# Summing the 16 states of a scan by adding DMA transfers into two tiles in turn, instead of additions on GpSimd

## Chip, cores, metric

One core of a Trainium2 chip. The time is the device time of one execution in microseconds (us); of several executions the median is given. A ratio is the mean time of one kernel's fast runs over the mean of the kernel before's fast runs of the same rounds, so it is not quite the ratio of the medians quoted.

## The reference, cut to what matters

Four images (128 channels, 64 x 64) pass through four layers: 0, attention; 1, two quantised convolutions; 2, a selective scan (Mamba) with group norm; 3, attention. The change touches the end of one step of layer 2:

```python
def step(h, inp):
    dt_t, B_t, C_t, x_t = inp
    dA = jnp.exp(dt_t[..., None] * A)                  # A: 256 channels x 16 states
    dBx = dt_t[..., None] * B_t[:, None, :] * x_t[..., None]
    h = dA * h + dBx
    y = jnp.einsum('bdn,bn->bd', h, C_t)               # the sum over the 16 states
    return (h, y)
...
y = ys + xc * D
y = y * jax.nn.silu(z)                                 # the gate
return y @ W_out
```

## The kernel before: the parts that matter

The kernel does one chunk of 512 pixels at a time, a *group* g; there are 32. In a group, states n = 0 to 15 follow each other; m = 16 g + n counts them, 512 in all. A tile of 128 x 1024 holds both halves of the 256 channels. For each state VectorE makes the product `hs = ud * B` (three buffers, L981), two scans over it (L989), and the readout `hs = hs * C` (L971), which is done one product later. GpSimd adds the readout to `y` (L1006) and, at the end of the group, multiplies by the gate `sz` (L1010).

Attention, convolutions and the scan are interleaved by a small list scheduler in the kernel (`Order`). Each part is a generator that yields, ahead of each instruction, its engine, an assumed time and what it needs; the scheduler writes the instructions in the order in which its model would start them. That order is then fixed for each engine. The numbers in `op(...)` make the order; they don't make the chip wait.

```python
def scans():
    for m in range(NM):
        g, n = divmod(m, DS)
        need = [("add", m - 3)] if m > 2 else []
        yield op("DVE", 1.25, ("bc", m), ("ud", g), *need, port=True)
        ud = live["in", g][1]
        hss[m] = hs = pair("hs", "hs", 3)              # three buffers
        nc.vector.tensor_mul(hs, ud, bcs[m][:, 0:1, :].to_broadcast([P, 2, TB]))   # L981
        ...
        if m:
            yield op("DVE", 1.22, ("last", m - 1), port=True)
            readout(m - 1)                             # L971, in place in hs
        for h in range(2):
            yield op("DVE", 1.26, ("da", m, h))
            nc.vector.tensor_tensor_scan(hs[:, h, :], ...)                         # L989

def additions():
    for m in range(NM):
        g, n = divmod(m, DS)
        yield op("POOL", 2.36, ("c", m), ("y", g))
        y = live["in", g][2]
        nc.gpsimd.tensor_tensor(y, y, hss.pop(m), ALU.add)                         # L1006
        mark("add", m)
        if n == DS - 1:
            yield op("POOL", 2.4, ("sz", g))
            nc.gpsimd.tensor_tensor(y, y, live.pop(("sz", g)), ALU.mult)           # L1010
            mark("gated", g)

def preparation():                                     # z of group g - 1, inputs of group g
    ...
    need = [("gated", g - 2)] if g > 1 else []
    for h in range(2):
        yield op("PE", 0.8, *need, ("begun", g - 1), bank=True)
        if h == 0:
            live["sz", g - 1] = sz = pair("sz", "sz", 1)                           # one buffer
        ps = product(...)                                                          # L738, z
        yield op("ACT", 0.69)
        nc.scalar.activation(sz[:, h, :], ps, AF.Copy, scale=1.0 / LEVELS)         # L761
```

B and C of a state come to all partitions by a 512 KB transfer from HBM, `bc` (three buffers, issued by SyncE, L941).

Of the kernel before, what the change touches and what calls it, by code (L numbers as in the profile page):

```python
# [16 lines left out]
ALU = mybir.AluOpType  # L17
# [28 lines left out]
class Order:  # L46
# [16 lines left out]
    @staticmethod  # L63
    def op(engine, time, *needs, bank=False, table=None, port=False, lag=0.0):
        return engine, time, needs, bank, table, port or engine == "POOL", lag
# [6 lines left out]
    def mark(self, *key):  # L72
        self.marks[key] = self.end
# [59 lines left out]
def conv_seq_kernel(ctx: ExitStack, tc: tile.TileContext, i: dict, out: bass.AP):  # L133
    nc = tc.nc
# [15 lines left out]
    def gtile(name):  # L150
        return ps_g.tile([P, TB], F32, tag="g", name=name)
# [14 lines left out]
    for c in range(NTB // 2):  # L166
# [3 lines left out]
            out=staged[0, c],  # L170
            in_=i["x"][0].rearrange("c (k r) w -> c k (r w)", r=ROWS)[:, 2 * c : 2 * c + 2],
# [167 lines left out]
    op, mark, release = order.op, order.mark, order.release  # L339
# [389 lines left out]
    stats, live, bcs, das, hss = {}, {}, {}, {}, {}  # L729

    def pair(name, tag, bufs):
        return mam.tile([P, 2, TB], F32, tag=tag, name=name, bufs=bufs)
# [266 lines left out]
        readout(NM - 1)  # L999

    def additions():
        for m in range(NM):
            g, n = divmod(m, DS)
            yield op("POOL", 2.36, ("c", m), ("y", g))
            y = live["in", g][2]
            nc.gpsimd.tensor_tensor(y, y, hss.pop(m), ALU.add)  # L1006
            mark("add", m)
            if n == DS - 1:
                yield op("POOL", 2.4, ("sz", g))
                nc.gpsimd.tensor_tensor(y, y, live.pop(("sz", g)), ALU.mult)  # L1010
                mark("gated", g)

    with tc.manual_schedule():
        for rank, chain in (
            (1, parts()),
            (1, convolutions()),
            (1, preparation()),
            (1, output()),
            (1, lasts()),
            (3, energies()),  # L1020
            (4, exponentials()),
            (4, products()),
            (3, decays(0)),
            (3, decays(1)),
            (3, scans()),
            (3, additions()),
            (3, fetches()),
            (3, images()),
        ):
            order.add(rank, chain)  # L1030
        order.run()
# [9 lines left out]
    g = gtile("ok_t")  # L1041
# [470 lines left out]
```

## Time and profile before

| | before |
|---|---|
| time, median of 2 | 3792.51 us (3791.74 to 3793.28) |
| TensorE / VectorE / ScalarE / GpSimd busy | 92 / 78 / 66 / 35% |
| first product to last readout (the recurrence), by the trace | 259 to 3365 us |
| VectorE idle in that stretch | 208 us |
| DMA share from 285 to 3300 us | 0.38 |

How to read it: up to 259 us and from 3365 us on attention runs nearly alone and TensorE is the bound. Between, TensorE and VectorE are both above 90% in one fixed order. The lines are shown in the prediction (VectorE's idle time, 205 us there, is 208 by the trace).

### The profile page before, as it was taken

What the parts mean: (1) busy time and instruction counts of PE and PEld (TensorE: products, weight loads), DVE (VectorE), ACT (ScalarE), POOL (GpSimd) and SP (SyncE); (2) the same over time, 40 slices, a digit from 0 to 9 for tenths busy, and PEclk for the clock granted to TensorE, in tenths of its full rate; (3) what the DMA queues carried; (4) which work ended last, traced back from release to release, by engine and by line L of the source; (5) the groups of instructions that cost most, each with busy time, mean ns of one, the idle gap of its engine ahead of it and who ended that gap; (6) DMA issues with size and microseconds to landing.
All of it is one profiled execution on the core that took longest, in us unless ns stands there. A gap on an engine that the chain in (4) does not pass through costs nothing.

```text
span 3780.8 us, 72475 instructions
## 1 busy us (share of the span) xinstructions
PE 3462.1 (92%) x30839; PEld 2258.3 (60%) x30839; DVE 2963.8 (78%) x2824; ACT 2512.8 (66%) x3658; POOL 1316.0 (35%) x568
## 2 busy tenths in 40 slices
PE   5999988999989999889998999999898988999998
PEld 3766656666656666645555666665454555556665
DVE  2039999999989999999998999989998888960000
ACT  2357767777776767677777777776776677764443
POOL 0004434444424444434443443443444444430000
PEclk8999999999999999999999999999999999999999
DMA  2013333333433333433443333333433433331000
GB/s 69 1 38 95 92 110 99 86 97 93 111 100 91 93 91 98 116 93 95 109 121 109 97 90 80 96 106 86 120 99 97 123 92 104 102 89 36 15 13 16
DMA packets 203662, 327.92 MB, mean 87 GB/s; under 512 B 50608, under 2 KB 53440, under 8 KB 203328
## 3 DMA queue, kind: packets, MB, share of 16 engines
q1 hardware_dynamic: 196384, 322.09, 31.8%
q8 instruction: 243, 3.98, 0.4%
q10 hardware_dynamic: 6944, 1.10, 0.2%
q14 instruction: 91, 0.75, 0.1%
HBM read 304.27 MB, written 18.87 MB: 85 GB/s over the span
## 4 chain that ended last, share of the span: by engine, by line
PE 60%; DVE 23%; ACT 11%; issue 5%; DMA 2%; ACTq 0%; DVEq 0%; SPq 0%
PE us L544 24%; PE e L491 13%; DVE hs L989 9%; PE us L554 8%; DVE hs L981 4%; DVE hs L971 3%; ACT da L954 2%; ACT p L507 2%; PE conv L649 2%; PE xh L738 2%; PE sc L614 1%; PE proj L462 1%; PE proj L420 1%; PE yo L868 1%; PE sc L601 1%
## 5 line engine op out<-in xcount | busy, mean ns | idle before, releaser
L1006 POOL TENSOR_TENSOR y<-y,hs 128x1024 f32<-128x1024 f32 x512 | 1216.6, 2376 | 2050.1 <-DVE hs L971 2022.7
L544 PE MATMUL us<-p,v 128*32 128x256 f32 (+1 forms) x12288 | 1537.2, 390 | 125.0 <-ACT p L507 125.0
L544 PEld LDWEIGHTS us<-p,v 128*32 128x32 f32 (+1 forms) x12288 | 1009.6, 138 | 564.8 <-issue 171.6
L507 ACT ACTIVATE p<-e 128x1024 f32<-128x1024 f32 x1024 | 1002.4, 1019 | 430.3 <-PE e L491 258.5
L989 DVE TENSOR_TENSOR_SCAN hs<-da,hlast,hs 128x512 f32<-128x512 f32 x896 | 1102.9, 1264 | 40.8 <-ACT da L954 40.5
L954 ACT ACTIVATE da<-dt,amat 128x512 f32<-128x512 f32 x1024 | 702.0, 691 | 271.1 <-DVE hs L989 263.7
L971 DVE TENSOR_TENSOR hs<-hs,bc 128x1024 f32<-128x1024 f32 x512 | 669.2, 1307 | 40.1 <-ACT hlast L964 39.6
L981 DVE TENSOR_TENSOR hs<-ud,bc 128x1024 f32<-128x1024 f32 x512 | 656.6, 1282 | 0.2
L554 PE MATMUL us<-p,ones 128*32 128x256 f32 x8192 | 544.1, 383 | 0.0
L491 PE MATMUL e<-it,v 64*128 64x256 f32 x4096 | 530.2, 398 | 14.0 <-ACT p L507 12.5
L491 PEld LDWEIGHTS e<-it,v 64*128 64x128 f32 x4096 | 382.2, 191 | 162.2 <-issue 89.7
L610 DVE RECIPROCAL rall<-sc 128x4 f32<-128x4 f32 x64 | 11.5, 179 | 529.2 <-PE sc L601 529.2
L554 PEld LDWEIGHTS us<-p,ones 128*32 128x32 f32 x8192 | 236.6, 110 | 209.1 <-issue 67.7
L491 PEld LDWEIGHTS e<-it,j 64*128 64x128 f32 x2048 | 140.9, 189 | 102.9 <-issue 69.5
L491 PE MATMUL e<-it,j 64*128 64x256 f32 x2048 | 195.5, 309 | 6.9 <-ACT p L507 5.9
L964 ACT COPY hlast<-hs 128x2 f32<-128x2 f32 x448 | 85.6, 191 | 130.8 <-DVE hs L989 125.0
L989 DVE TENSOR_TENSOR_SCAN hs<-da,hs 128x512 f32<-128x512 f32 x128 | 150.3, 1206 | 1.8 <-ACT da L954 1.7
L738 PEld LDWEIGHTS <-w 128*128 128x128 bf16 x576 | 51.7, 98 | 106.5 <-issue 58.4
L738 PE MATMUL xh<-x,w 128*128 128x512 fp8e4 x384 | 94.6, 383 | 3.8 <-DVE x L709 2.8
L1010 POOL TENSOR_TENSOR y<-y,sz 128x1024 f32<-128x1024 f32 x32 | 95.8, 2995 | 2.5
L601 PEld LDWEIGHTS sc<-sel,ss 128*128 128x128 f32 x512 | 65.0, 190 | 40.2 <-issue 18.3
L601 PE MATMUL sc<-sel,ss 128*128 128x1 f32 x512 | 73.1, 254 | 14.5 <-ACT ss L582 10.4
(158 smaller groups left out, 2517.9 us busy)
## 6 DMA issues: line engine op xcount, KB each, us to landing
bc<-bc_d SPq DMA_DIRECT2D x512, 512.0 KB, 4.8
x_in<-in_x SPq DMA_DIRECT2D x16, 512.0 KB, 4.7
xpad<-in_x SPq DMA_DIRECT2D x32, 256.0 KB, 3.2
x_d<-yo SPq DMA_DIRECT2D x32, 256.0 KB, 2.5
x_in<-x_d SPq DMA_DIRECT2D x16, 512.0 KB, 6.1
o<-x_d SPq DMA_DIRECT2D x32, 256.0 KB, 5.3
out<-o SPq DMA_DIRECT2D x32, 256.0 KB, 2.7
bc_d<-xd SPq DMA_DIRECT2D x64, 32.0 KB, 1.7
```

The lines of the kernel that those rows point to most:

```text
L491: nc.tensor.matmul(e[k % 4 // 2][:, k % 2, k // 4, :], lhsT=jts[s][row : row + D3, col : col + P], rhs=its[s][row : row + D3, c * CB : (c ...
L507: nc.scalar.activation(p, es[t][h], AF.Exp)
L544: nc.tensor.matmul(us[rows, 0, :], lhsT=vts[s][:, 8 * q + k, cols], rhs=ps[t, h][:, k % 2, k // 4, :], start=False, stop=False,)
L554: nc.tensor.matmul(us[32 * m : 32 * m + 32, 1, :], lhsT=ones[:, 0:32], rhs=ps[t, m // 2][:, k % 2, k // 4, :], start=False, stop=q == NQ - ...
L601: nc.tensor.matmul(sc[:, k : k + 1], lhsT=ss[:, k * P : (k + 1) * P], rhs=sel4, start=True, stop=True,)
L738: nc.tensor.matmul(g, lhsT=w3[:, k // len(rhs), lhs[k % len(rhs)] : lhs[k % len(rhs)] + P], rhs=x[:, rhs[k % len(rhs)]], start=(k == 0), s ...
L954: nc.scalar.activation(da, live["in", g][0][:, h, :], AF.Exp, scale=amat[:, h, n : n + 1])
L971: nc.vector.tensor_mul(hs, hs, bcs.pop(m)[:, 1:2, :].to_broadcast([P, 2, TB]))
L981: nc.vector.tensor_mul(hs, ud, bcs[m][:, 0:1, :].to_broadcast([P, 2, TB]))
L989: nc.vector.tensor_tensor_scan(hs[:, h, :], das.pop((m, h)), hs[:, h, :], hlast[:, n, h : h + 1] if g % NTB else 0.0, ALU.mult, ALU.add,)
L1006: nc.gpsimd.tensor_tensor(y, y, hss.pop(m), ALU.add)
L1010: nc.gpsimd.tensor_tensor(y, y, live.pop(("sz", g)), ALU.mult)
```

## The change

The intent: to keep GpSimd's additions off the SBUF port that VectorE's two-input instructions need (page and trace for this are in the prediction). A DMA transfer can add into its destination, and takes GpSimd for its issue alone (0.86 us in the trace after). Successive additions to one tile have to wait for each other, so they go to two tiles, `y` and `odd`, in turn, and GpSimd adds the two at the group's end.

```diff
     def additions():
+        odd = None
         for m in range(NM):
             g, n = divmod(m, DS)
-            yield op("POOL", 2.36, ("c", m), ("y", g))
+            need = [("add", m - 2)] if m > 1 else []
+            if n == 1 and g:
+                need.append(("gated", g - 1))
+            yield op("POOL", 1.0, ("c", m), ("y", g), *need, lag=4.0)
             y = live["in", g][2]
-            nc.gpsimd.tensor_tensor(y, y, hss.pop(m), ALU.add)
+            if n == 1:
+                odd = pair("odd", "odd", 1)
+            nc.gpsimd.dma_start(
+                out=odd if n % 2 else y,
+                in_=hss.pop(m),
+                accum_op=ALU.bypass if n == 1 else ALU.add,
+            )
             mark("add", m)
             if n == DS - 1:
+                yield op("POOL", 2.4, ("add", m - 1), ("add", m))
+                nc.gpsimd.tensor_tensor(y, y, odd, ALU.add)
                 yield op("POOL", 2.4, ("sz", g))
                 nc.gpsimd.tensor_tensor(y, y, live.pop(("sz", g)), ALU.mult)
                 mark("gated", g)
```

## The prediction

> **What bounds the kernel now.** I began with the page's busy line and its forty slices: is one engine the bound all through?
>
> ```profile
> PE 3462.1 (92%) x30839; PEld 2258.3 (60%) x30839; DVE 2963.8 (78%) x2824; ACT 2512.8 (66%) x3658; POOL 1316.0 (35%) x568
> PE   5999988999989999889998999999898988999998
> DVE  2039999999989999999998999989998888960000
> POOL 0004434444424444434443443443444444430000
> DMA  2013333333433333433443333333433433331000
> ```
>
> TensorE is at nine tenths throughout. VectorE is too, but from slice 3 to slice 34 alone, while the recurrence of layer 2 runs; before and after it attention runs alone. GpSimd has slack everywhere, DMA more. The table of windows puts numbers on the two stretches (columns: PE, PEld, DVE, ACT and POOL busy, clock, DMA share, GB/s):
>
> ```profile
> 285.00:3300.00 3015.00, 2763.89 (x23284) 1801.68 (x23283) 2809.51 (x2586) 2175.79 (x3249) 1267.37 (x526) 0.97 0.38 100
> 3300.00:3781.00 481.00, 463.72 (x5942) 288.74 (x5940) 89.34 (x115) 219.83 (x266) 35.40 (x15) 1.00 0.11 35
> ```
>
> In the first, VectorE (93%) and TensorE (92%) bound it together in one fixed instruction order: 251 us of TensorE idle is all there is to win. In the second only TensorE counts, and it is nearly full. How much of VectorE is on the path, the chain of work that ended last tells:
>
> ```profile
> PE 60%; DVE 23%; ACT 11%; issue 5%; DMA 2%; ACTq 0%; DVEq 0%; SPq 0%
> ```
>
> 23% of 3781 us is 870 us, of 2964 us that VectorE is busy: a microsecond of VectorE taken or given, spread evenly, moves the end by about 0.29 us.
>
> Then the groups of the change itself, and the instances of the two products by line (min/median/max ns):
>
> ```profile
> L1006 POOL TENSOR_TENSOR y<-y,hs 128x1024 f32<-128x1024 f32 x512 | 1216.6, 2376 | 2050.1 <-DVE hs L971 2022.7
> L971 DVE TENSOR_TENSOR hs<-hs,bc 128x1024 f32<-128x1024 f32 x512 | 669.2, 1307 | 40.1 <-ACT hlast L964 39.6
> L981 DVE TENSOR_TENSOR hs<-ud,bc 128x1024 f32<-128x1024 f32 x512 | 656.6, 1282 | 0.2
> L1010 POOL TENSOR_TENSOR y<-y,sz 128x1024 f32<-128x1024 f32 x32 | 95.8, 2995 | 2.5
> L971 DVE TENSOR_TENSOR hs<-hs,bc x512: 1160/1212/3408, 264.2 to 3363.4; 128x1024 f32<-128x1024 f32 x171
> bc<-bc_d SPq DMA_DIRECT2D x512, 512.0 KB, 4.8
> ```
>
> The 512 additions (2.38 us each) wait for VectorE: 2023 us idle, released by L971. So GpSimd is not a bound: its 1217 us are worth nothing by themselves. They cost only where they hold up VectorE. L971 shows that: most take 1212 ns, the longest 3408.
>
> **What the skill says.** "SBUF — State Buffer", Who interferes with whom: a VectorE instruction with two SBUF inputs contends with a GpSimd instruction that reads SBUF, and the later one blocks for the whole of the other. The trace agrees: of L971's instances 22 take 3.28 to 3.41 us, and by the timeline each of these starts about a microsecond after the gating product L1010. "DMA: Bandwidth & Descriptors", Anatomy of one DMA: a GpSimd-issued transfer takes about 2.0 us + bytes/436e3; for 512 KB (524,288 bytes) that is 3.2 us. The transfers of that size here (bc, issued by SyncE from HBM) land after 3.4 us at best and 4.8 at the median, so a loaded queue costs 1.6 more. "Collectives: The Full Stack", The bandwidth ceiling: a reducing transfer reads two sources on one ring, and ran at about half the copy's rate. No transfer that adds is in this trace. "DMA: Bandwidth & Descriptors", Two DMAs through the same engine are not ordered: only the completion semaphore orders dependent transfers. That is why the change waits for the addition two states back and keeps two tiles; no run here shows it.
>
> **The change part by part.** Removed: 512 GpSimd additions. Added on GpSimd: 512 issues of a 512 KB transfer within SBUF, of which 480 add and 32 (the first into the odd tile) copy, and 32 additions y + odd, 32 x 2.4 = 76 us, off the path. Moved: the instruction order itself, since the scheduler now books 1.0 us of GpSimd, not 2.36; the listing of VectorE's instructions differs on most rows, with the same work in it.
>
> What VectorE gets back. L971: (1307 - 1212) x 512 = 49 us. L981: instances that lie beside no addition take about 1.205 us in the timeline, so (1282 - 1205) x 512 = 39 us. The same sum over the smaller groups (L684, L407, L627, L701, L673, L844) gives 30. Together 118. But the 49 of L971 are blocks by L1010 at the end of each group of 16 states, which stays, and now has another addition in front of it. I keep 39 + 30 = about 70 us. On the path: 70 x 0.29 = 20 us faster.
>
> What it must pay. Tile hs has three buffers, so the product of state m + 3 waits until addition m has read hs of state m. Before, that was done 2.4 us after L971. The time there is can be read off the timeline of VectorE:
>
> ```profile
> 3303.94 1.20 DVE L981 TENSOR_TENSOR hs<-ud,bc 128x1024 f32<-128x1024 f32 x1
> 3305.06 1.21 DVE L971 TENSOR_TENSOR hs<-hs,bc 128x1024 f32<-128x1024 f32 x1
> 3306.20 2.45 DVE L989 TENSOR_TENSOR_SCAN hs<-da,hlast,hs 128x512 f32<-128x512 f32 x2
> 3308.57 1.30 DVE L981 TENSOR_TENSOR hs<-ud,bc 128x1024 f32<-128x1024 f32 x1
> 3309.79 1.21 DVE L971 TENSOR_TENSOR hs<-hs,bc 128x1024 f32<-128x1024 f32 x1
> 3310.93 2.44 DVE L989 TENSOR_TENSOR_SCAN hs<-da,hlast,hs 128x512 f32<-128x512 f32 x2
> 3313.30 1.59 DVE L981 TENSOR_TENSOR hs<-ud,bc 128x1024 f32<-128x1024 f32 x1
> ```
>
> The readout of state m ends at 3306.27, the product of m + 3 starts at 3313.30: 7.0 us. Over all 509 such pairs the least is 6.9, the lower quartile 7.0, the median 8.1 and the 95th percentile 16.2. A transfer that lands within 7 us of its readout costs nothing, one slower by a microsecond hits a third of the states. One state comes every 6.06 us on average, so the wait for the addition two states back is harmless.
>
> At the end of each group GpSimd stands: it waits for the last two landings, then 2.4 + 3.0 us of arithmetic, and only then issues the next group's first transfer, so that one lands late whatever the rest does. I replayed the trace's readout times with a landing time L after the issue and this stop. The stalls add up to 0 us of VectorE for L = 4, 25 for 5, 67 for 6, 123 for 7, 256 for 8, 400 for 9.
>
> So L decides. From bc's 4.8 us; 0.4 more for GpSimd's first byte (the first page's table has 1 us against 0.6); a second read of 512 KB, 1.2 us at that page's rate or 1.95 at the rate here. (The hardware queue took 31.8% of 3781 us for 322 MB; bc's 268 MB are 83% of it, 1000 us, over 512.) L is an estimate of 6.4 to 7.2 us. The DMA share of 0.38 grows by 2 x 1.2 to 2 x 1.95 us per 6.06 us, that is to between 0.78 and 1.02, so queues lengthen: 6.5 to 8, I choose 7. That is 123 us of stall. VectorE has 205 us of idle time in the stretch that takes up some of it, but a stall strikes an in-order engine when it is the late one, so I count 0.45 of it rather than 0.29 (a choice): 55 us. The inputs of each attention stage share the same engines; DMA is 2% of the chain, 76 us, and a sixth more is 12.
>
> Sum: 3792.5 - 20 + 55 + 12 = 3840 us.
>
> **The rivals.** First, the landing is quick (5 us or less): no stall beyond 25 us, VectorE gains 70 or, if the boundary blocks go too, 118, and the end comes 10 to 34 us sooner, 3760 to 3785. For it: an uncontended 3.4 us exists here. Against: this transfer moves twice as much past the same engines. Second, DMA becomes the bound: with 3.9 us for an addition, 1.95 for bc and about 0.35 for the rest, 6.2 us per state exceed 6.06, and in the runs of 4.7 us per state it is far over. Then L rises to 8 or 9 and the stalls to 256 to 400 us, times 0.45 to 0.6: 3910 to 4030. For it: nothing measured here says that an addition is cheaper than twice a copy. Against: packets that stay in SBUF may be quicker than bc's from HBM. Third, removing the lock frees the whole phase, because VectorE and TensorE both run above 90%: 118 us of VectorE at full worth is 3675. Against it: 0.29 on the chain, and the gate's blocks that remain. Fourth, the new order alone moves things by some 20 us either way. The late gate (about 8 us later) should not hold TensorE much: in the trace before the output product L868 starts mostly 9 to 20 us after L1010 ends.
>
> **Range and chances.** L below 6 (a quarter): 3760 to 3805. L from 6 to 7.5 (two fifths): 3805 to 3865. Above (a third): 3865 to 4030. So 3745 to 4010 holds eight in ten. Faster by over 2% means under 3717 and needs the third rival: 0.07. Slower by over 2% means over 3868: 0.38. Within: 0.55.
>
> **What would show it.** The table of DMA issues should give the adding transfers a landing of 6.5 to 8 us and bc's above 4.8, with a DMA share of 0.75 or more in the middle slices. L981, which waited 0.2 us in all, should now wait for GpSimd's transfers, 70 to 180 us in total, most of it two to four states into a group. L981's mean should fall to near 1.21 us; L971 should keep its long instances. The recurrence should end 20 to 80 us later than 3364. If L981 shows no such wait, the payment is wrong; if the landing is 7 us and the time still falls, my weight of 0.45 is. Landings under 5 us or above 9 put the time outside my middle.

A note for the reader: the "first page" and "that page" of the paragraph "So L decides" are the Trainium skill's "DMA: Bandwidth & Descriptors"; the 1 us and 0.6 us stand in its section Latency and other measured facts. No run here measures the first byte.

## The result

3994.72 us (3990.83 to 3998.61, 2 runs): 202 us more, ratio 1.0533 (1.0508 to 1.0559), slower. The prediction had 48 us more.

The page of the kernel after, the lines that answer to those of before:

```profile
PE 3529.6 (88%) x30835; PEld 2286.5 (57%) x30839; DVE 2932.1 (73%) x2824; ACT 2517.3 (63%) x3655; POOL 620.5 (16%) x600
DVE  2048988898888988888788888888888788881000
DMA  2037767777777776877677777777777787782000
q0 software_dynamic: 73728, 268.47, 33.1%
DMA 32%; PE 31%; DVE 19%; issue 9%; ACT 5%; POOL 3%; ACTq 0%; SPq 0%; POOLq 0%; DVEq 0%
bc<-bc_d SPq DMA_DIRECT2D x512, 512.0 KB, 5.4
y<-hs POOLq DMA_DIRECT2D x256, 512.0 KB, 7.6
```

GpSimd's 1217 us of additions have become a DMA queue that takes 33.1% of the DMA engines, as much as all other transfers. VectorE has lost 32 us of work (2963.8 to 2932.1), but its slices fell from 9 to 8: it waits. DMA, 2% of the chain that ends last before, is 32% of it now. By the trace the recurrence ends at 3604 instead of 3365 us; what follows is 393 us instead of 416, so the whole loss lies in the recurrence.

From 285 to 3300 us (PE, PEld, DVE, ACT, POOL busy, clock, DMA share, GB/s), against 2763.89 us of TensorE and 2809.51 of VectorE in the same stretch before:

```profile
285.00:3300.00 3015.00, 2666.13 (x21571) 1737.28 (x21572) 2587.16 (x2421) 2045.29 (x3037) 550.07 (x515) 0.95 0.76 173
```

Who waits for the transfers, from the instances of the product L981 (us, times) and from the waits of all engines (us in total, times, longest):

```profile
  DMA y<-hs: 180.0, 123
  DMA odd<-hs: 62.9, 73
  DMA bc<-bc_d: 4.9, 4
```

```profile
ACT sz L761 <- POOL y L1023: 30.8, 11, 5.2
```

The product waited 0.2 us in all before; now 249.1 us by the page's group line, nearly all of it for the transfers. And ScalarE waits for the gate's multiplication. How both arise shows best at one group's end, in the timeline of the kernel after (start, duration, engine, line, then in brackets the idle time before it and what ended it; L1021 is y + odd, L1023 the gate, L1013 the transfers):

```profile
1520.48 1.22 DVE L981 TENSOR_TENSOR hs<-ud,bc 128x1024 f32<-128x1024 f32 x1 [0.54 <-DMA odd<-hs]
...
1520.60 3.31 POOL L1021 TENSOR_TENSOR y<-y,odd 128x1024 f32<-128x1024 f32 x1 [8.48 <-DMA odd<-hs]
...
1521.63 3.37 DVE L971 TENSOR_TENSOR hs<-hs,bc 128x1024 f32<-128x1024 f32 x1
...
1523.99 3.20 POOL L1023 TENSOR_TENSOR y<-y,sz 128x1024 f32<-128x1024 f32 x1
...
1527.15 0.87 POOL L1013 DMA_DIRECT2D y<-hs  x1
...
1527.23 0.60 ACT L761 ACTIVATE sz<-z 128x512 f32<-128x512 f32 x1 [4.61 <-POOL y L1023]
...
1527.88 0.81 PE L738 MATMUL z<-x,w 128*128 128x512 fp8e4 x3 [3.08 <-ACT sz L761]
...
1532.97 1.23 DVE L981 TENSOR_TENSOR hs<-ud,bc 128x1024 f32<-128x1024 f32 x1 [5.60 <-DMA y<-hs]
```

GpSimd stood for 8.48 us until the last landing, then did y + odd and the gate. Meanwhile (i) ScalarE stood for 4.61 us, since it may overwrite `sz` only after the gate, (ii) TensorE waited behind it for 3.08 us, (iii) the readout L971 was blocked and took 3.37 us instead of 1.22, and (iv) the first transfer of the new group went out only at 1527.15, so that the product which needs its `hs` buffer stood for 5.60 us. From the group's last readout to the end of its gate the traces have a median of 5.8 us before and 14.4 after.

### The profile page after: what moved, and what is told of

Same layout as the page of the kernel before. It is cut to its first block, busy times and chain, and to the rows that moved or that the text cites.

```text
span 3996.8 us, 72519 instructions
## 1 busy us (share of the span) xinstructions
PE 3529.6 (88%) x30835; PEld 2286.5 (57%) x30839; DVE 2932.1 (73%) x2824; ACT 2517.3 (63%) x3655; POOL 620.5 (16%) x600
## 3 DMA queue, kind: packets, MB, share of 16 engines
q0 software_dynamic: 73728, 268.47, 33.1%
## 4 chain that ended last, share of the span: by engine, by line
DMA 32%; PE 31%; DVE 19%; issue 9%; ACT 5%; POOL 3%; ACTq 0%; SPq 0%; POOLq 0%; DVEq 0%
DMA y<-hs 18%; PE us L544 12%; DMA odd<-hs 10%; PE e L491 6%; DVE hs L981 5%; DVE hs L989 5%; DVE hs L971 5%; PE us L554 4%; PE conv L649 2%; POOL y L1023 2%; POOL y L1021 2%; DMA o<-x_d 2%; PE proj L420 1%; PE proj L462 1%; PE sc L614 1%
## 5 line engine op out<-in xcount | busy, mean ns | idle before, releaser
L981 DVE TENSOR_TENSOR hs<-ud,bc 128x1024 f32<-128x1024 f32 x512 | 634.4, 1239 | 249.1 <-DMA y<-hs 180.0
L971 DVE TENSOR_TENSOR hs<-hs,bc 128x1024 f32<-128x1024 f32 x512 | 675.0, 1318 | 36.5 <-ACT hlast L964 36.2
L491 PE MATMUL e<-it,v 64*128 64x256 f32 x4096 | 541.0, 405 | 14.3 <-ACT p L507 13.3
L1013 POOL DMA_DIRECT2D y<-hs x256 | 220.3, 860 | 1548.1 <-DVE hs L971 1471.4
L1013 POOL DMA_DIRECT2D odd<-hs x256 | 214.7, 839 | 1208.9 <-DVE hs L971 1138.1
L1021 POOL TENSOR_TENSOR y<-y,odd 128x1024 f32<-128x1024 f32 x32 | 89.9, 2809 | 233.3 <-DMA odd<-hs 187.6
L738 PE MATMUL z<-x,w 128*128 128x512 fp8e4 x192 | 56.7, 407 | 47.8 <-ACT sz L761 46.4
```

Source lines behind the costliest of these rows:

```text
L491: nc.tensor.matmul(e[k % 4 // 2][:, k % 2, k // 4, :], lhsT=jts[s][row : row + D3, col : col + P], rhs=its[s][row : row + D3, c * CB : (c ...
L738: nc.tensor.matmul(g, lhsT=w3[:, k // len(rhs), lhs[k % len(rhs)] : lhs[k % len(rhs)] + P], rhs=x[:, rhs[k % len(rhs)]], start=(k == 0), s ...
L971: nc.vector.tensor_mul(hs, hs, bcs.pop(m)[:, 1:2, :].to_broadcast([P, 2, TB]))
L1013: nc.gpsimd.dma_start(out=odd if n % 2 else y, in_=hss.pop(m), accum_op=ALU.bypass if n == 1 else ALU.add,)
L1021: nc.gpsimd.tensor_tensor(y, y, odd, ALU.add)
```

## The experiments

The theories at the start: **A**, the `hs` buffer comes free late (landing 7.6 us after issue, 8.0 after the readout, where the steady pace leaves 7.0); **B**, the doubled DMA load by itself; **C**, the new instruction order. **D**, the single `sz` buffer, came up after the second batch. "Old order" means that TensorE, VectorE and ScalarE have exactly the instruction sequence of the kernel before, "new order" that of the changed kernel. Kernels that leave out work are wrong; apart from e12_copy (relative error 0.34) the comparison with the reference let them pass all the same, so it is too coarse for this sum: they are used for their times only, and "correct" is weak evidence for the transfers' sums too.

| run | order | what | median us | ratio (95%) |
|---|---|---|---|---|
| the change | new | transfers, 3 hs, 1 sz | 3994.72 | 1.0533 (1.0508 to 1.0559) |
| e1_hs4 | new | 4 hs | 3906.00 | 1.0312 (1.0295 to 1.0330) |
| e2_pool_two | new | additions on GpSimd | 3936.63 | 1.0392 (1.0374 to 1.0409) |
| e3_half | new | half the bytes | 3856.92 | 1.0175 (1.0153 to 1.0196) |
| e4_load | old | additions on GpSimd, idle transfers beside | 3822.18 | 1.0082 (1.0061 to 1.0102) |
| e5_free_old | old | no additions | 3736.17 | 0.9868 (0.9850 to 0.9886) |
| e6_free_new | new | no additions | 3783.01 | 0.9984 (0.9977 to 0.9990) |
| e7_old_order_hs3 | old | transfers, 3 hs, 1 sz | 4059.04 | 1.0709 (1.0691 to 1.0728) |
| e8_old_order_hs4 | old | 4 hs | 3986.69 | 1.0522 (1.0505 to 1.0540) |
| e9_old_hs3_sz2 | old | 2 sz | 4007.68 | 1.0569 (1.0551 to 1.0587) |
| e10_before_hs4 | old | control: before with 4 hs | 3791.56 | 1.0004 (0.9995 to 1.0013) |
| e11_tail4 | old | last 4 states on GpSimd, 4 hs | 3878.26 | 1.0245 (1.0217 to 1.0272) |
| e12_copy | new | copies instead of additions | 3852.64 | one run, state unknown |
| e13_old_hs4_sz2 | old | 4 hs, 2 sz | 3817.57 | 1.0078 (1.0058 to 1.0099) |
| e14_new_hs4_sz2 | new | 4 hs, 2 sz | 3868.49 | 1.0224 (1.0193 to 1.0254) |
| e15_free_lag0 | third | no additions | 3796.57 | 1.0020 (1.0013 to 1.0027) |
| e16_free_210 | fourth | no additions | 3774.95 | 0.9968 (0.9956 to 0.9980) |

### First batch: buffer, transfers, bytes, load

**e1_hs4.** A fourth buffer, in space taken from two other tiles; the scheduler's numbers are untouched:

```diff
-                        us = att.tile([P, TB], F32, tag="us", name="us", bufs=2)
-                        ss = att.tile([P, TB], F32, tag="ss", name="ss", bufs=2)
+                        us = att.tile([P, TB], F32, tag="us", name="us", bufs=1)
+                        ss = att.tile([P, TB], F32, tag="ss", name="ss", bufs=1)
-            hss[m] = hs = pair("hs", "hs", 3)
+            hss[m] = hs = pair("hs", "hs", 4)
```

> The changed kernel with a fourth hs buffer (space from us and ss, one buffer each instead of two); the instruction order on every engine stays that of the change. Theory A, the buffer: hs is freed 8.0 us after the readout where 7.0 are to be had, and VectorE waits 249 us for it; a fourth buffer gives some 11.7 us, so L981's wait falls from 249 to under 60 us and the time to 3790 to 3850 us. Theory B, the load: twice the DMA traffic itself (share 0.76) slows the inputs of the attention stages and everything behind them; the wait at L981 may go, but the time stays above 3900. Theory C, the new order is at fault: the time stays near 3990.

3906.0 us: 89 us of the 202 are gone. The product's waits:

```profile
  DMA bc<-bc_d: 55.1, 49
  DMA y<-hs: 33.9, 9
```

The wait for `hs` fell from 243 to 34 us (what is left are group ends), and a wait for `bc` of 55 us took a part of its place. So A is true, and far from all: 3906 lies above A's range, and by its letter B's "above 3900" holds.

**e2_pool_two.** The additions back on GpSimd, in the new order, into the two tiles:

```diff
-            nc.gpsimd.dma_start(out=odd if n % 2 else y, in_=hss.pop(m), accum_op=...)
+            t = odd if n % 2 else y
+            if n == 1:
+                nc.gpsimd.tensor_copy(t, hss.pop(m))
+            else:
+                nc.gpsimd.tensor_tensor(t, t, hss.pop(m), ALU.add)
```

> The changed kernel's order and its two tiles, but the additions done on GpSimd again (the first into the odd tile as a copy): it undoes the transfers alone. Theory A and B: back to 3770 to 3820 us, as before, with 32 more GpSimd additions of 2.4 us off the path. Theory C (the order made for 1.0 us of GpSimd is a bad one, or the stop at the end of each group): 3850 us or more.

3936.6 us, which A and B had excluded: undoing the transfers alone gives back only 58 us. But the test is not a clean one of the order. VectorE's busy time is 3048.4 us here, against 2963.8 in the kernel before with the same instructions: an order made for 1.0 us of GpSimd puts VectorE's two-input instructions beside additions that take 2.4. The order had to be tested without any additions.

**e3_half.** Each transfer moves one of the two channel halves (wrong); a `memset` per group on GpSimd, not shown, clears the other half of `odd`:

```diff
-            nc.gpsimd.dma_start(out=odd if n % 2 else y, in_=hss.pop(m), ...)
+            t, hs = odd if n % 2 else y, hss.pop(m)
+            nc.gpsimd.dma_start(out=t[:, 0, :], in_=hs[:, 0, :], ...)
```

> The changed kernel, each transfer moving the first 512 of the 1024 columns only (wrong result on purpose; the order is the same). Half the bytes: the landing should fall from 7.6 to 5 to 6 us, below the 7.0 us there are. Theory A: L981 waits under 60 us in all, time 3780 to 3840 us. Theory B: half the added traffic takes back half of the 202 us, some 3890 us. The relation need not be linear under A, it must be near linear under B.

The landing falls to 6.0 us, the waits at L981 to 31 us, as A has it:

```profile
y<-hs POOLq DMA_DIRECT2D x256, 256.0 KB, 6.0
```

But the time, 3857, is above A's range and below B's 3890. The wait goes away with the landing time; something else of some 70 us does not.

**e4_load.** The kernel before, plus transfers that nobody waits for. To make room for their two tiles, `us` and `ss` have one buffer each, as in e1:

```diff
             nc.gpsimd.tensor_tensor(y, y, hss.pop(m), ALU.add)
             mark("add", m)
+            nc.gpsimd.dma_start(out=spare[m % 2], in_=<4 KB per partition of w3>, accum_op=ALU.add)
```

> The kernel before, with its additions on GpSimd, plus 512 adding transfers of 512 KB in turn into two spare tiles that nothing reads, issued after each addition (source: a constant tile). Same result as before. It puts the load of the change on the DMA engines without anyone waiting for a landing. Theory A: 3790 to 3830 us (bc lands within its slack; the inputs of the attention stages land 1 us later). Theory B: 3880 us or more, with DMA share near 0.75 and TensorE idle for inputs and VectorE for bc.

3822.2 us, 1.0082: a DMA share of 0.82 from 285 to 3300 us costs 31 us (0.82%) at the old order's pace if nobody waits for the landing of these transfers. B as the main cause is out.

### Second batch: the order by itself

**e5_free_old and e6_free_new.** No additions at all, in either order (wrong); `hss.pop(m)` stands in place of the addition or transfer, and in the new order y + odd goes too.

> The kernel before in its own order, with the 512 additions left out (wrong result on purpose; the gate stays): nobody adds, nothing lands, hs is free after its readout. It shows what the additions on GpSimd cost the kernel before, and so the most that the change can win in the old order. From the trace before: 70 us of VectorE that waits for GpSimd go, 49 stay with the gate. If VectorE's time counts fully in this stretch: 3720 us. With my weight of 0.29: 3770 us.

> The same in the changed kernel's order: no additions, no transfers, no y + odd (wrong result on purpose). The difference to the run in the old order is the order alone, without locks, stalls or load. Theory C' (the new order is worse by itself): 40 to 80 us above the old order without additions, that is 3790 to 3840 us. Theory A alone: within 15 us of it.

3736.2 and 3783.0 us. Without additions the old order is 54 us (1.3%) faster, and the new order takes 47 of these back before anything is transferred. But leaving out the additions takes away more than their work: nothing makes the gate wait for the readouts any longer. The gate L1010 of the kernel before, and of e5:

```profile
L1010 POOL TENSOR_TENSOR y<-y,sz x32: 2340/3222/3252, 361.1 to 3367.2; 128x1024 f32<-128x1024 f32 x32
L1010 POOL TENSOR_TENSOR y<-y,sz x32: 2345/2378/4190, 311.5 to 3258.2; 128x1024 f32<-128x1024 f32 x32
```

In e5 the gate ends 67 us (median) before its group's last readout, in e6 65 us, where it ended 5.8 us after it. So its blocks of L971 at the group's start are mostly gone too (L971's mean is 1246 ns, not 1307, against the expectation that they stay), and ScalarE never waits to overwrite `sz`. The 54 us are therefore the worth of the additions and of the gate's place together; no run has one without the other. The 47 us compare two kernels that both lack this wait.

**e7_old_order_hs3 and e8_old_order_hs4.** The transfers in the old order: `additions()` of the kernel before with its `op("POOL", 2.36, ...)`, the `dma_start` of the change in it, and y + odd ahead of the gate; then the same with the buffers of e1.

> The transfers of the change, three hs buffers, but the instruction order of the kernel before on TensorE, VectorE and ScalarE (the scheduler is still told of 2.36 us on GpSimd). If stall and order add up: the changed kernel less 50 to 80 us, 3915 to 3945. If the stall hides what the order costs (the wait at L981 takes the place of waits for ScalarE and TensorE): within 25 us of 3995.

> The same with four hs buffers. Theory A plus C': stall gone, old order, only the load is left: 3790 + 31 of load - 20 to 50 of freed VectorE, some 3780 to 3815 us, against 3906 in the new order. Theory A with a load effect that is greater where VectorE waits for bc (55 us in the new order with four buffers): 3830 to 3870. Without an order effect: 3900.

4059.0 and 3986.7 us: my theories had said faster than in the new order (3995 and 3906) or, at worst, about the same, and both are slower. In e8 the product waits only 39 us, for `bc`. The waits of all engines in e7 have the reason:

```profile
ACT sz L761 <- POOL y L1018: 180.8, 30, 9.9
PE z L738 <- ACT sz L761: 152.7, 28, 9.8
```

ScalarE's next write to `sz` stands 6 us for nearly every gate (L1018 is the gate here), TensorE's second z product behind it, and everything that ScalarE has yet to do in its fixed order, exponentials, last columns, decays, behind that. In the changed kernel it was 31 us: its scheduler had been told of the landing time, and put z later. (Where nothing has to wait, the write to `sz` comes 8.8 us after the last readout of the group before in the old order, e5, and 13.5 in the new one, e6.) That is D.

### Third batch: the sz buffer, a control, a repair, the price of adding

**e9_old_hs3_sz2.** e7 with a second `sz` buffer (space from `us` and `ss`): `pair("sz", "sz", 1)` becomes `pair("sz", "sz", 2)`.

> The transfers in the old order with three hs buffers, and two sz buffers instead of one (space from us and ss). In the old order ScalarE waits 181 to 189 us to overwrite sz, because the gate that reads it ends 14.5 us after the last readout instead of 5.8. Theory D, the late gate holds ScalarE by the single sz buffer, and ScalarE's order holds the rest: that wait goes to under 10 us and the time from 4059 to 3900 to 3960 us; the wait for hs at L981 stays near 240 us. If the wait for sz was harmless: within 25 us of 4059.

4007.7 us, 51 less; the wait for the gate is gone from ScalarE's list. The time is above the range that D gave. The product's waits for `hs` rose from 236 to 266 us: where one wait is taken away, the other takes a part of its place.

**e10_before_hs4.** The edit of e1 in the kernel before.

> Control: the kernel before, with the fourth hs buffer and single us and ss buffers, nothing else. It should be the kernel before within 0.5% (3775 to 3810 us), for hs is there in time already and us and ss are evicted 16 to 21 us apart. If it is slower than that, the runs with four buffers carry this cost too.

1.0004: the extra `hs` buffer and the single `us` and `ss` do nothing by themselves in the old order without transfers.

**e11_tail4.** In the old order, four hs buffers:

```diff
+            if n == 12:
+                nc.gpsimd.tensor_tensor(y, y, odd, ALU.add)
+            if n < 12:
+                nc.gpsimd.dma_start(...)
+            else:
                 nc.gpsimd.tensor_tensor(y, y, hss.pop(m), ALU.add)
```

> A repair, in the old order: the first 12 states of each group by transfers into the two tiles, then y + odd and the last 4 states on GpSimd, four hs buffers. The gate should end about 6 us after the last readout as before, so no wait for sz (under 20 us) and none for hs (under 30). What is left is three quarters of the load (24 us of the 32) and less of the lock: 3755 to 3800 us, that is within 1% of the kernel before. If load and waits for bc cost more than thought: 3820 to 3850.

3878.3 us, a miss. The gate is on time again (5.8 us after the last readout, as before) and only 24 us of waits for `bc` are left at L981, but VectorE is busy for 2989.3 us, 26 more than before although a quarter of the additions are left on GpSimd, and the load is there. By the trace 44 of the 47 us that L971 gained are in the readouts of states 13 to 15; that the tail's additions, late behind y + odd, block them is likely and not tested.

**e12_copy.** `accum_op=ALU.bypass` for all (wrong), one run. ("The skill's page" in the expectation is "Collectives: The Full Stack", The bandwidth ceiling.)

> The changed kernel with every transfer a copy instead of an addition (wrong result on purpose): the price of adding in a transfer. If the second read costs what the skill's page says, the landing falls from 7.6 us to 6.0 to 6.5, the queue's share of the DMA engines from 33% to about half of it, and L981's wait from 249 to under 130 us; if the addition costs nothing by itself, the landing stays above 7.2.

The queue of the transfers, and their landings:

```profile
q0 software_dynamic: 73728, 268.47, 17.3%
```

```profile
DMA to landing us min/median/max: 2.8/5.9/8.8
```

For the changed kernel the same view has:

```profile
DMA to landing us min/median/max: 4.5/7.6/11.5
```

The same bytes, the same number of packets, 1.9 times the share (33.1 to 17.3%). As the spans differ, time is the better measure: 33.1% of 3996.8 us is 1323 us, 17.3% of 3850.8 us is 666. Adding costs as much DMA time again as copying, and 1.7 us of landing both at best and at the median.

The median hides one thing. A readout frees its `bc` along with its `hs`: SyncE issues the next `bc` 0.03 us after it, and GpSimd its transfer 0.30 us after it (medians), so that the two run side by side. In the changed kernel the 458 transfers that went out within 1 us of a `bc` landed after 7.65 us (median), the other 54 after 5.85; in e12 it is 5.88 and 3.15. In e4, where the same kind of adding transfer goes out 2.46 us after the readout, it landed after 6.0. So 1.6 to 1.8 of the 7.6 us seem to come of starting together with `bc`; that is a comparison of transfers, and no run moved one of the two.

### Fourth batch: both releases repaired; how much an order moves by chance

**e13_old_hs4_sz2 and e14_new_hs4_sz2.** Four hs and two sz buffers, in either order. For the space a tile of attention (`h`) shares the buffer of `sp`; no run has this sharing alone:

```diff
-            h = att.tile([P, 2 * TB], F32R, tag="h", name="h", bufs=1)
+            h = mam.tile([P, 2 * TB], F32R, tag="sp", name="h", bufs=1)
```

> The transfers in the old order with four hs buffers and two sz buffers together (the space from us, ss and h, which shares sp's). If late releases and load are the whole: no wait for hs or sz, 3736 without additions + 32 of load + some 40 of waiting for bc = 3790 to 3830 us, where either repair alone gave 3987 and 4008. If something else is lost (gate, output): 3870 or more.

> The same two repairs in the changed kernel's own order. From 3906 with the fourth hs buffer alone; the wait for sz was 52 us there and should go: 3840 to 3880 us, that is the old order repaired plus about 47 of the order. If the sz wait cost nothing in this order: 3895 to 3910.

3817.6 and 3868.5 us, both in the range that was expected. In the old order the two repairs together take 241 us off e7 (4059), where alone they took 72 and 51: each hid what the other cost. The product's waits in e13:

```profile
  DMA bc<-bc_d: 42.9, 45
  DMA y<-hs: 26.5, 15
```

**e15_free_lag0 and e16_free_210.** No additions, two more orders: the new numbers with `lag=0.0` for `lag=4.0`; the old numbers with 2.1 for 2.36.

> No additions (wrong result on purpose), the order made with the change's numbers except that the landing time of 4 us is booked as 0. If the order is worse because it is made for late landings and a late gate: near the old order's 3736 (3725 to 3755). If any other order costs as much, by chance: 3760 to 3800.

> No additions (wrong result on purpose), the old order's numbers but 2.1 us for an addition instead of 2.36: a small change that means nothing on the chip here. It shows how much an order moves the time by chance: if orders are alike, 3725 to 3750; if chance alone is worth tens of microseconds, up to 3790.

3796.6 and 3775.0 us against 3736.2 and 3783.0. None of the four has an addition or a transfer to wait for; they differ in order alone, and by up to 60 us. So a loss like the 47 us of the new order needs no landing times for a cause: the three other sets of numbers all gave 39 to 60 us more than the old one, which is the best of the four. They lose it in different places, though: the recurrence ends at 3316 us in e5, 3391 in e6, 3322 in e15 and 3306 in e16, and what follows takes 418, 388, 473 and 466 us. In e6 the recurrence itself is slower; in e15 and e16 more attention is left over for the end. No version with a correct sum beats the kernel before; the best that keeps all transfers (e13) is 0.8% slower than it.

## Why the prediction was wrong

The ladder in the new order (medians; ratios in the table):

| step | us | from |
|---|---|---|
| no additions, old order (e5) | 3736 | 54 below the kernel before |
| the new order, no additions (e6) | 3783 | +47 |
| transfers, no late release (e14) | 3868 | +85 |
| one sz buffer (e1) | 3906 | +38 |
| three hs buffers (the change) | 3995 | +89 |

By the ratios each step differs by up to 6 us. The steps stand in this sequence; in another the shares would differ, as e7 to e9 show. Steps two and five are one change each (the space for the fourth `hs` buffer costs nothing in e10). Step three also brings back the gate's wait for the readouts and y + odd, and frees space by sharing `h`; step four undoes that sharing along with the second `sz` buffer.

The measured time lies inside the range of 3745 to 4010 us, but in the tail that I had kept for a saturated DMA queue; the forecast of 48 us more was off by a factor of four. The stall that it named is real, but only 89 of the 202 us. Its sum failed in four terms: the load of the DMA engines (12 us; the step that holds it is 85), the order (0, give or take 20; 47), the late gate (0; 38) and the stall (55; 89). The gain went the other way (20; 54, with the gate's place in it). Step by step:

- **Landing time: right; DMA share: at the low end.** 7 us chosen from 6.5 to 8, measured 7.6 (and 0.3 from readout to issue); share 0.78 to 1.02 worked out, 0.76 measured.
- **Wait for hs: right in kind, and half in size.** The replay gave 123 us for L = 7 and 256 for 8; it was 243 (249 with `bc`). The fourth product of the group, which needs the buffer of the first transfer after the stop, has 88 us of it; the replay for 7 us has nearly all 123 there. The rest is spread over the group, because a landing 8.0 us after the readout is later than the 7.0 us of the steady pace: the prediction had left out the 0.3 us of issue and taken 0.6 too little for the landing. The weight of 0.45 was not the fault: the fourth buffer returned 89 us for 209 us less of waiting for `hs`, 0.43, though 55 us of waiting for `bc` came in its place. The term of 55 us should have been 89.
- **Gain on VectorE: 70 us expected, 32 measured** (busy time 2963.8 to 2932.1). L981's mean fell to 1239 ns, not 1210. L971 kept its long instances (3399 at most), as expected. Without any additions, and with the gate elsewhere, VectorE is at 2869.9 (e5).
- **"The late gate (about 8 us later) should not hold TensorE much": the step whose mechanism was missed.** The gate came 8.6 us later, and the output product waited 11.6 us for it in all: that much was right. I had asked only who needs the gate's *result*. I had not asked whose *buffer* the gate frees. `sz` has one buffer, its next writer is ScalarE, and ScalarE's order holds the rest: 38 us here (e14 to e1), and in an order that doesn't know of the late gate far more (e8 to e13: 169).
- **"12" for the shared DMA engines: too small.** e4 has 31 us with nobody waiting; with VectorE's pace no longer held up, `bc` came late for 47 us in e14. The 85 us of that step hold both, the group ends (33 us), TensorE's waits for stage inputs and the gate's return to the group's end; I did not separate them, so how they share it stays open.
- **"The new order alone moves things by some 20 us either way": too small.** 47 us here, 39 and 60 in e16 and e15. The recurrence ended 239 us later, not 20 to 80.
- **TensorE's clock, which the prediction left out.** The granted clock fell from 0.973 to 0.95, and TensorE's busy time rose by 67 us for the same matmuls. Over the runs it goes with the time (0.970 in e5, 0.961 in e14, 0.939 in e7), but in the attention at the end, with TensorE 99% busy, it is 1.00 in both kernels (3500 to 3700 us before, 3700 to 3900 after). The clock records in the traces tell more: after the first 100 us it is granted at half for stretches of 3 to 17 us, 187 us in all before and 381 after. Of the pauses of TensorE of 3 us or more, 20 of 21 are followed within 7 us of their end by the start of such a stretch before, and 34 of 38 after; at times picked at random that would be 12 and 22%. So a pause comes first, and a wait seems to cost TensorE some time twice. That the pause is the cause is inferred from this order in time; no run changed pauses alone. The steps of the ladder contain it.

## What to carry to other kernels

An asynchronous operation that is "off the engines" still holds its source and destination until it lands: for each instruction that becomes later, list who writes next to every buffer it *reads*, not only who reads what it writes. When two late releases hide each other, repair both at once before judging either. In a fixed order made by a scheduler, a change of its numbers alone can be worth more than the change under test, so test the order with the disputed work taken out, and look at what else stops waiting when that work is gone: here it was the gate.

## What the Trainium skill lacked or had wrong

- "DMA: Bandwidth & Descriptors": it names adding as a thing that a GpSimd-issued transfer can do, without a cost. Here: 512 KB within SBUF landed 7.6 us after issue when adding and 5.9 when copying (median, beside `bc`; 4.5 and 2.8 at best); GpSimd's issue took 0.86 us when adding and 0.53 when copying. Its fit for a copy (Anatomy of one DMA; an estimate of 3.2 us for 512 KB) agrees with the 3.15 us of the 44 copies of e12 that went out more than 1 us away from a `bc`, and not with the median of all.
- "Collectives: The Full Stack", The bandwidth ceiling: it has the halved rate of a reducing transfer for collectives alone. A transfer within SBUF shows the same: 1323 us of DMA time against 666 for the same bytes copied.
- "SBUF — State Buffer", Who interferes with whom: it states the lock and not its worth in a whole kernel. Here all 512 additions, with the gate's place at the group's end, cost 54 us of 3790 (e5), and 94 us of VectorE's busy time.
- No page has the chain shown here: a buffer whose reader waits for a DMA, so that its next writer and all that follows in that engine's order wait too: one `sz` buffer cost 38 us in one order and 169 in the other.
